# First layer: where a borrowed PSUM bank's piece is copied out, and the next one begun, in slots 5 and 6

## The chip, the cores and the metric

One core of a Trainium2 chip runs the whole program: TensorE (PE in the profile), VectorE (DVE), ScalarE (ACT), GpSimd (POOL) and the DMA queue of SyncE (SP). The metric is the device time of one execution in microseconds (us). The kernel before took 17000.62 us, the median of three runs (16998.64 to 17003.07).

## The reference

Eight images of 48 x 48 x 96 pass four layers; each layer adds its output to its input, after a group norm of the input. Cut to what matters:

```
def step(h, inp):                       # layers 0, 2 and 3: a selective scan along the pixels
    u, dl, Bv, Cv = inp
    dA = jnp.exp(dl[..., None] * A)
    h = h * dA + (dl * u)[..., None] * Bv[:, :, None, :]
    y = jnp.einsum('bkdn,bkn->bkd', h, Cv)
    return (h, y)
...
h = jnp.transpose(_upsample_rfft(xc), (0, 2, 3, 1))   # layer 1: a pointwise MLP on twice the resolution
h = h @ W1.T + b1
h = coef[:, 0] + coef[:, 1] * h + coef[:, 2] * (h * h)
h = h @ W2.T + b2
...                                                    # low pass, every second pixel
x = x + _L0_conv_ref(_gn(x), ...)
x = x + _L1_conv_ref(_gn(x), ...)
x = x + _L2_conv_ref(_gn(x), ...)
x = x + _L3_conv_ref(_gn(x), ...)
```

In each scan layer an image is read in four directions, with 192 channels and 16 states.

## The kernel before, in words

**Stages.** `ss2d("l0")` computes layer 0, `lines` layer 2, `ss2d("l3")` layer 3. Layer 1, the MLP, has no stage of its own. It is a *guest* (class `Guest`): a generator (`items`) cuts it into small pieces, and the pieces are worked off beside layers 0 and 2 as soon as an image of layer 0 is done.

**Blocks, turns and slots.** A direction of an image is cut into five blocks of 480 or 384 pixels, so a scan layer has 8 x 4 x 5 = 160 blocks. A block has four turns (0 to 3), and a turn has two slots, so a block has slots 0 to 7. Each turn runs three scans on DVE (`scan`, L337), of two groups of 128 rows each. A scan needs the products that DVE or POOL made (`make_dbu`, L305) and a pair of exponentials that ACT wrote to PSUM (`make_da`, two ACTIVATEs of L329 for one scan). The PSUM buffers of these pairs are two, so ACT can be at most one pair ahead of the scan in work. After a scan, POOL multiplies the states (`make_hc`, L343), and PE sums them (`reduce`, L363 and L365).

**The order is written out by hand.** The program turns the scheduler off (`manual_schedule`): each engine runs its instructions in the order in which the code issues them. In turn t the loop of `scans` issues: scan of pair 0, exponentials of pair 1, scan of pair 1, exponentials of pair 2, the copy of B to PSUM for an odd slot (`copy_b`, L286), the first `aside`, then `begin`, `make_hc`, *the first pair of exponentials of the next turn*, scan of pair 2, another `copy_b`, and the second `aside`. In turn 3 the next turn is turn 0 of the next block.

**What an aside does.** `aside(at)` (L407 to L425) first lets the guest *settle*: ACT copies out of PSUM what the pieces begun in the slot before have left there. Then it issues loads, a step of the side work (`side`: the convolution that prepares the next image, or the layer norm and output of the last one), the stage steps of the block that comes next (`stage1`), and at last `guest.turn`.

**The guest's turn** (L1022) issues DMAs whose time has come, earns one credit a slot (two at most), and begins one piece for each credit and free PSUM bank: PE matmuls now, the ACT copy put on a list (`put`) for the next settle. In layer 0 two banks can be free (L766):

```
guest.banks = lambda slot, clear: (["side"] if clear else []) + (["s1"] if slot in (2, 5, 6) else [])
```

The bank `side` belongs to the side work and is lent when that is between two steps (`clear`). The bank `s1` belongs to the stage steps, which use it so in each block: step `s0` in slot 7 (PE, L721), its copy in slot 1 (ACT, L726), `raw` in slots 3 and 4 (PE, L711), `biased` in slots 4 and 5 (ACT, L715). In slot 6 comes the Softplus (ACT, L739), with a table load before it and one before the exponentials that follow. So `s1` is lent in slots 2, 5 and 6.

**Pieces and their lines** (PE, then the ACT copy of its result): raising the height L1145 and L1147; `widen` L1174 and L1176; `hidden` L1181 and L1183; `narrow` L1192 and L1194, of 18 matmuls or of 12; `slim` L1203 and L1200; `lower` L1235, L1237 and L1240.

Of the kernel before, what the change touches and what calls it, by code (L numbers as in the profile page):

```python
# [29 lines left out]
NG = 8  # L30
# [72 lines left out]
def vss_stack_kernel(ctx: ExitStack, tc: tile.TileContext, i: dict, out: bass.AP):  # L103
# [120 lines left out]
    def scans(dirs, order, restart, on_pool, a, pools, ps, stage1, opening, done, side, tail, ahead=None, guest=None):  # L224
# [30 lines left out]
        def load_dd(b, half):  # L255

            t = pools["dd"].tile([P, 3 * 2 * WMAX], F32, tag="dd", name="dd")
            nc.sync.dma_start(t[:, :6 * b.m], b.dd[half].unsqueeze(1).to_broadcast([32, 4, 6 * b.m]))
            b.got[half] = t[:, :6 * b.m].rearrange("p (g t m) -> p g t m", g=3, t=2)

        def load_bc(t):

            b, slot = blocks[t // NG], t % NG
            sg = ORDER[slot][1]
            other = t - slot + NG - 1 - slot
            n = min(free, key=lambda n: free[n])
            free[n] = other
            r = bufs[n]
            rows4 = b.bcd[8 * sg:8 * sg + 8, :].rearrange("(s w) n -> s (w n)", w=2)
            nc.sync.dma_start(r[:, LEAD:LEAD + 2 * b.n], rows4.unsqueeze(0).to_broadcast([32, 4, 2 * b.n]))  # L270

            lo, hi = LEAD - b.at.start, LEAD + b.n
            bcs[t] = bcs[other] = r[:, lo:hi + b.at.start], r[:, hi:hi + b.n]
# [17 lines left out]
        def make_dbu(t, engine):  # L291

            if t >= NG * len(blocks):
                return
            b, slot = blocks[t // NG], t % NG
            if t // 2 not in dbus:
                dbus[t // 2] = rooms[t // 2 % (NG // 2)]
            cut = 3 - on_pool.get(slot, 0)
            lo, hi = (0, cut) if engine is nc.vector else (cut, 3)
            if lo == hi:  # L300
                return
            o = units(dbus[t // 2], b, 3 * (slot % 2) + lo, 3 * (slot % 2) + hi)[:, :, b.by]
            du = b.got[ORDER[slot][0]][:, lo:hi, 1, b.by]
            by = (bps[t] if engine is nc.vector else bcs[t][0])[:, b.by]
            engine.tensor_mul(o, du, by.unsqueeze(1).to_broadcast([P, hi - lo, by.shape[1]]))  # L305
# [13 lines left out]
        def make_da(t, pair):  # L319
            if t >= nt:  # L320
                return
            b, q = turns[t]
            da = ps("da", 2, 1024)
            das[t, pair] = da
            for u in (2 * pair, 2 * pair + 1):
                half, sg = ORDER[2 * q + u // 3]
                ci = half * 12 + sg * 3 + u % 3
                at = (u - 2 * pair) * b.m
                nc.scalar.activation(da[:, at:at + b.m], b.got[half][:, u % 3, 0, :], AF.Exp, scale=a[:, b.k, ci:ci + 1])  # L329

        def scan(t, pair):
            b, q = turns[t]
            da = das.pop((t, pair))[:, :2 * b.m]
            db = dbus[t][:, 2 * pair * b.m:(2 * pair + 2) * b.m]
            if b.back:
                da, db = da[:, ::-1], db[:, ::-1]
            nc.vector.tensor_tensor_scan(db, da, db, 0.0, ALU.mult, ALU.add)  # L337

        def make_hc(t, sub):
            b, q = turns[t]  # L340
            n = b.n
            h = units(dbus[t], b, 3 * sub, 3 * sub + 3)[:, :, b.at]
            nc.gpsimd.tensor_mul(h, h, bcs.pop(2 * t + sub)[1].unsqueeze(1).to_broadcast([P, 3, n]))  # L343

        def finish(at):
            while ends:
                b, half = ends.pop()
                for n, step in done(b, half, ys.pop((b, half))):
                    later.setdefault(at + n, []).append(step)

        def reduce(t, sub):

            b, q = turns[t]
            n = b.n
            half, slot = q // 2, 2 * (q % 2) + sub
            if slot == 0:
                ys[b, half] = ps("y", 1)
                lhsT, rhs = opening(b, half)
                nc.tensor.matmul(ys[b, half][:, :n], lhsT=lhsT, rhs=rhs, start=True, stop=False)  # L359
            y = ys[b, half]  # L360
            hc = units(dbus[t], b, 3 * sub, 3 * sub + 3)
            for g in range(3):
                nc.tensor.matmul(y[32 * g:32 * g + 32, :n], lhsT=wc["red"][:, :32], rhs=hc[:, g, b.at], start=False, stop=(slot == 3))  # L363

            nc.tensor.matmul(y[DH:, :n], lhsT=wc["red"][:, 32:], rhs=hc[:, 2, b.at], start=False, stop=(slot == 3))  # L365
            if slot == 3:
                ends.append((b, half))
            if sub == 1:
                dbus.pop(t)
# [3 lines left out]
        def plan(b, at):  # L373
            b.got = {}
            sources(b, pools)
            for n, step in stage1(b).items():
                steps.setdefault(at + n, []).append(step)

        def run(t):
            for step in steps.pop(t, []):  # L380
                step()
# [25 lines left out]
        def aside(at):  # L407

            nblk, slot = at // NG + 1, at % NG
            if guest:  # L410
                guest.settle()
            if nblk < len(blocks):
                for n, of in enumerate(LOAD_BC):
                    if of == slot:
                        load_bc(NG * nblk + n)
                if slot in load_in:
                    load_dd(blocks[nblk], load_in.index(slot))
            clear = next(beside, True)
            run(at)
            for step in later.pop(at, []):  # L420
                step()
            while tail:
                tail.pop(0)()
            if guest:
                guest.turn(slot, clear)  # L425

        for t, (b, q) in enumerate(turns):
            at, nblk = 2 * t, t // (NG // 2)
            if q == 0:
                if nblk + 3 < len(blocks):  # L430
                    plan(blocks[nblk + 3], at + NG)
                if b.k == order[0] and b.first:
                    beside = side(b.job)
            scan(t, 0)
            if t > 0:
                make_hc(t - 1, 1)
            make_dbu(at + 2, nc.vector)
            make_da(t, 1)
            make_dbu(at + 2, nc.gpsimd)
            make_dbu(at + 3, nc.gpsimd)  # L440
            if t > 0:
                reduce(t - 1, 0)
            scan(t, 1)
            make_da(t, 2)
            copy_b(at + 3)
            make_dbu(at + 3, nc.vector)
            if t > 0:
                reduce(t - 1, 1)
            aside(at)
            begin(t + 2)  # L450
            make_hc(t, 0)
            make_da(t + 1, 0)
            scan(t, 2)
            copy_b(at + 4)
            finish(at + 1)
            aside(at + 1)
            if q == NG // 2 - 1 and b.k == order[-1] and b.last:
                for _ in beside:
                    while tail:
                        tail.pop(0)()  # L460
# [534 lines left out]
    class Guest:  # L995
# [15 lines left out]
        def tile(self, shape, name):  # L1011
            return self.pool.tile(shape, F32, tag=f"g_{name}", name=f"g_{name}")

        def settle(self):
            while self.pending:
                self.pending.pop(0)()

        def put(self, p, step, behind):
            step(p)
            self.pending.append(lambda: behind(p))  # L1020

        def turn(self, slot, clear):  # L1022
            ready, self.soon = [f for n, f in self.soon if n <= 1], [(n - 1, f) for n, f in self.soon if n > 1]
            for step in ready:
                step()
            self.credit = min(self.credit + self.rate, 2.0)
            if self.wait:
                self.wait -= 1
                return
            banks = self.banks(slot, clear)  # L1030
            while True:
                self.item = self.item or next(self.work)
                kind, *of = self.item
                if kind == "idle":
                    self.item = None
                    return
                if kind == "wait":
                    self.item, self.wait = None, of[0] - 1
                    return
                if kind == "do":  # L1040
                    self.item = None
                    of[0]()
                    continue
                if not banks or self.credit < 1.0:
                    return
                self.item = None
                self.credit -= 1.0
                self.put(self.psum(banks.pop(0)), *of)

        def items(self):  # L1050
            room = self.room
# [206 lines left out]
    guest = Guest(stack, x1, x2)  # L1258
# [98 lines left out]
```

## Time and profile before

| | |
|---|---|
| median of the runs | 17000.62 us (16998.64 to 17003.07) |
| the profiled execution, its own time | 17010.73 us |
| its span, first to last instruction | 17007.9 us |
| mean granted TensorE clock | 0.854 |
| layer 0 with guest pieces beside it | about 1250 to 5755 us of the span |

The page gives each engine's busy time and the groups of instructions by line. "Idle before" is the time in which that engine stood idle just ahead of the group's instructions, with what ended it. A timeline lists instructions in order of time: start, length, engine, line, operation, output and inputs, shape, how many follow each other, and in brackets the idle time before. Reductions (L363, L365) are left out below where they say nothing.

### The profile page before, as it was taken

The numbers are of one execution on the slowest core, as the hardware profiler recorded it, in microseconds if no ns is written. First come the engines' busy times: TensorE is split into PE (matmuls) and PEld (weight loads), VectorE is DVE, ScalarE is ACT, GpSimd is POOL, SyncE is SP. The second block draws the span as 40 slices with busy tenths as digits, with TensorE's granted clock in tenths as the row PEclk, the third lists the DMA queues.
The fourth block names the chain that finished last, engine by engine and source line by source line (L and its number), as shares of the span: only waits on it lengthen the run. The fifth ranks groups of instructions, "written<-read, shape, count | busy, mean of one in ns | idle before, by whom it ended". The sixth has DMA issues, their size and how long they took to land.

```text
span 17007.9 us, 172189 instructions
## 1 busy us (share of the span) xinstructions
PE 13000.3 (76%) x53740; PEld 4643.6 (27%) x53740; DVE 15774.2 (93%) x9680; ACT 13824.5 (81%) x20812; POOL 15185.0 (89%) x7999
## 2 busy tenths in 40 slices
PE   6778887888787777777777777776777777777776
PEld 1223232333332333233323332221222222222221
DVE  7999999999999799999999999997999999999998
ACT  6878878888787688888888888886877878878876
POOL 7998989998889788888888888887999999999998
PEclk7878888889898789889989998887888878878887
DMA  4555555564555444544454444444545455555554
GB/s 149 180 170 172 180 163 182 171 185 169 173 172 179 141 153 167 167 161 164 158 171 159 158 166 160 160 156 139 180 168 181 173 170 176 176 172 176 175 176 143
DMA packets 931143, 2844.03 MB, mean 167 GB/s; under 512 B 396668, under 2 KB 464988, under 8 KB 803406
## 3 DMA queue, kind: packets, MB, share of 16 engines
q1 hardware_dynamic: 930222, 2833.03, 49.9%
q8 instruction: 422, 6.91, 0.2%
q14 instruction: 499, 4.09, 0.1%
HBM read 2384.40 MB, written 448.17 MB: 167 GB/s over the span
## 4 chain that ended last, share of the span: by engine, by line
POOL 24%; DVE 22%; ACT 21%; issue 18%; PE 10%; DMA 3%; SPq 1%; POOLq 0%; DVEq 0%; ACTq 0%
DVE dbu L337 15%; POOL dbu L343 14%; ACT ps_da L329 8%; POOL dbu L305 7%; DVE dbu L305 6%; ACT L329 3%; POOL dds L507 3%; PE ps_y L363 2%; ACT ps_b L286 1%; DMA bc<-bcd 1%; DMA dd<-dds 1%; PE ps_side L582 1%; PE ps_s L711 1%; ACT L739 1%; PE ps_sb L874 1%
## 5 line engine op out<-in xcount | busy, mean ns | idle before, releaser
L337 DVE TENSOR_TENSOR_SCAN dbu<-ps_da,dbu 128x968 f32<-128x968 f32 (+3 forms) x5760 | 11822.8, 2075 | 782.2 <-ACT ps_da L329 644.7
L343 POOL TENSOR_TENSOR dbu<-dbu,bc 128x1440 f32<-128x1440 f32 (+1 forms) x3840 | 10065.4, 2635 | 1486.5 <-DVE dbu L337 948.7
L329 ACT ACTIVATE ps_da<-dd,w_l_a 128x484 f32<-128x484 f32 (+3 forms) x11520 | 7419.0, 649 | 2395.5 <-DVE dbu L337 2166.1
L363 PE MATMUL ps_y<-dbu,w_red 128*32 128x480 f32 (+1 forms) x23040 | 4282.5, 658 | 1806.8 <-POOL dbu L343 1744.4
L365 PE MATMUL ps_y<-dbu,w_red 128*32 128x480 f32 (+1 forms) x7680 | 4242.3, 658 | 0.0
L305 DVE TENSOR_TENSOR dbu<-dd,ps_b 128x962 f32<-128x962 f32 (+5 forms) x2720 | 3810.3, 1401 | 186.2 <-ACT ps_b L286 137.7
L305 POOL TENSOR_TENSOR dbu<-dd,bc 128x481 f32<-128x481 f32 (+3 forms) x2080 | 3883.9, 1883 | 0.0
L363 PEld LDWEIGHTS ps_y<-dbu,w_red 128*32 128x32 f32 x23040 | 708.5, 118 | 5244.5 <-POOL dbu L343 3767.7
L286 ACT COPY ps_b<-bc 128x482 f32<-128x482 f32 (+2 forms) x2560 | 1364.6, 533 | 116.5 <-DVE dbu L305 104.1
L582 PE MATMUL ps_side<-xpad,w_l_cw 128*128 128x480 f32 (+1 forms) x2880 | 1323.1, 597 | 46.7 <-ACT g_room L1183 16.4
L329 ACT ACT_TABLE_LOAD x993 | 1274.0, 1283 | 17.4
L711 PE MATMUL ps_s<-bcl,square 128*128 128x480 f32 (+1 forms) x1280 | 874.3, 773 | 231.3 <-ACT dds L715 82.6
L359 PE MATMUL ps_y<-big,eye 128*128 128x480 f32 (+1 forms) x960 | 745.5, 865 | 254.2 <-ACT big L762 249.7
L721 PE MATMUL ps_s<-big,square 128*128 128x480 f32 (+1 forms) x1280 | 844.5, 790 | 66.4 <-ACT g_room L1183 18.0
L507 POOL TENSOR_TENSOR dds<-dds,big 96x960 f32<-96x960 f32 (+1 forms) x320 | 706.7, 2209 | 123.3 <-ACT dds L739 120.4
L582 PEld LDWEIGHTS ps_side<-xpad,w_l_cw 128*128 128x128 f32 x2880 | 559.8, 205 | 789.3 <-issue 671.9
L874 PE MATMUL ps_sb<-xpad,square 128*128 128x480 f32 (+1 forms) x1280 | 613.6, 626 | 46.9 <-ACT g_room L1183 22.8
L365 PEld LDWEIGHTS ps_y<-dbu,w_red 128*32 128x32 f32 x7680 | 647.5, 117 | 0.0
L874 PE MATMUL ps_sa<-xpad,square 128*128 128x480 f32 (+1 forms) x1280 | 521.3, 548 | 0.0
L917 PE MATMUL ps_sa<-xpad,square 128*128 128x480 f32 (+1 forms) x320 | 251.5, 881 | 342.1 <-ACT g_room L1183 109.7
L762 ACT COPY big<-ps_y 96x480 f32<-96x480 f32 (+1 forms) x640 | 471.7, 737 | 39.0 <-PE ps_y L365 37.6
L711 PEld LDWEIGHTS ps_s<-bcl,square 128*128 128x128 f32 x1280 | 249.6, 239 | 759.5 <-ACT dds L715 327.2
(250 smaller groups left out, 12525.4 us busy)
## 6 DMA issues: line engine op xcount, KB each, us to landing
dd<-dd SPq DMA_DIRECT2D x512, 1452.0 KB
bc<-bcd SPq DMA_DIRECT2D x1536, 480.0 KB
dd<-dd SPq DMA_DIRECT2D x256, 1440.0 KB
dd<-dds SPq DMA_DIRECT2D x1536, 121.0 KB
dd<-dd SPq DMA_DIRECT2D x128, 1164.0 KB
bc<-bcd SPq DMA_DIRECT2D x384, 384.0 KB
dd<-dds SPq DMA_DIRECT2D x768, 120.0 KB
dd<-dd SPq DMA_DIRECT2D x64, 1152.0 KB
```

The source lines that it names most:

```text
L286: nc.scalar.copy(bps[t][:, :bcs[t][0].shape[1]], bcs[t][0])
L305: engine.tensor_mul(o, du, by.unsqueeze(1).to_broadcast([P, hi - lo, by.shape[1]]))
L329: nc.scalar.activation(da[:, at:at + b.m], b.got[half][:, u % 3, 0, :], AF.Exp, scale=a[:, b.k, ci:ci + 1])
L337: nc.vector.tensor_tensor_scan(db, da, db, 0.0, ALU.mult, ALU.add)
L343: nc.gpsimd.tensor_mul(h, h, bcs.pop(2 * t + sub)[1].unsqueeze(1).to_broadcast([P, 3, n]))
L363: nc.tensor.matmul(y[32 * g:32 * g + 32, :n], lhsT=wc["red"][:, :32], rhs=hc[:, g, b.at], start=False, stop=(slot == 3))
L365: nc.tensor.matmul(y[DH:, :n], lhsT=wc["red"][:, 32:], rhs=hc[:, 2, b.at], start=False, stop=(slot == 3))
L507: nc.gpsimd.tensor_mul(du, dt, u)
L582: nc.tensor.matmul(pu[:, :n], lhsT=flat[:, at:at + P], rhs=xpad[:, r0 + dy:r0 + dy + nr, dx:dx + W], start=(tap == 0), stop=(tap == 8))
L711: nc.tensor.matmul(got["p"][:, :n], lhsT=wide("dtw", (2 * b.k + half) * DH), rhs=b.bcl[:, :n], start=True, stop=True)
L721: nc.tensor.matmul(got["p"][:, :n], lhsT=wide("xp", (2 * b.k + half) * NBC), rhs=uall[:, half], start=(half == 0), stop=(half == 1))
L874: nc.tensor.matmul(got["u", half][:, :n], lhsT=wide("cw", at), rhs=shifted(off), start=(tap == 0), stop=(tap == 3))
```

## The change

Only layer 0 is touched, since the new branches need a guest and `restart` false; layer 2 has `restart` true, and layer 3 has no guest.

- In slot 6, `aside` settles all pending copies except those of the bank `s1`. It returns without the guest's turn, and hands `clear` to the loop.
- In the same turn (turn 3), after `begin`, `make_hc` and `make_da(t + 1, 0)`, the loop settles the rest (the copy of a piece begun in `s1` in slot 5), and then runs the guest's turn of slot 6.
- `put` takes the bank's name and keeps it beside the copy, so that `settle` can tell which to hold.

```
 def aside(at):
     if guest:
-        guest.settle()
+        guest.settle(("s1",) if slot == 6 else ())
...
+    if guest and slot == 6 and not restart:
+        return clear
     if guest:
         guest.turn(slot, clear)
...
-    aside(at)
+    clear = aside(at)
     begin(t + 2)
     make_hc(t, 0)
     make_da(t + 1, 0)
+    if guest and at % NG == 6 and not restart:
+        guest.settle()
+        guest.turn(6, clear)
     scan(t, 2)
     copy_b(at + 4)
...
-def settle(self):
-    while self.pending:
-        self.pending.pop(0)()
-
-def put(self, p, step, behind):
+def settle(self, held=()):
+    now = [step for bank, step in self.pending if bank not in held]
+    self.pending = [(bank, step) for bank, step in self.pending if bank in held]
+    for step in now:
+        step()
+
+def put(self, bank, step, behind):
+    p = self.psum(bank)
     step(p)
-    self.pending.append(lambda: behind(p))
+    self.pending.append((bank, lambda: behind(p)))
```

More of the change, by code (lines that the diff above doesn't have):

```diff
@@ L1047, in turn @@
                 self.credit -= 1.0
-                self.put(self.psum(banks.pop(0)), *of)
+                self.put(banks.pop(0), *of)
         def items(self):
```

## The prediction

> **What bounds the kernel now.** I read the page first, then sums by stretch, then the timelines of single blocks.
>
> ```profile
> PE 13000.3 (76%) x53740; PEld 4643.6 (27%) x53740; DVE 15774.2 (93%) x9680; ACT 13824.5 (81%) x20812; POOL 15185.0 (89%) x7999
> ...
> L337 DVE TENSOR_TENSOR_SCAN dbu<-ps_da,dbu 128x968 f32<-128x968 f32 (+3 forms) x5760 | 11822.8, 2075 | 782.2 <-ACT ps_da L329 644.7
> ```
>
> DVE is busy for 93% of the span, and more than half of its idle time (782.2 of some 1234 us) lies before scans; the exponentials on ACT end most of that. The same by stretch, the second being layer 0 with guests:
>
> ```profile
> 1310.00:5750.00 4440.00, 3611.91 (x16335) 1463.73 (x16334) 4069.17 (x2503) 3645.39 (x5725) 3974.26 (x2266) 0.86 0.54 173
> ```
>
> The columns are PE, PE weight loads, DVE, ACT, POOL, the granted clock, DMA. DVE idles 371 us, ACT 795, POOL 466: DVE sets the pace, and what holds DVE up is what can be won. Sorting the scans of layer 0 by their place in the block (counted over the trace's scan records), of the twelve, the first scan of turn 0 carries 154.5 us of idle, the first of turn 2 53.6, the first two of turn 3 50.3 and 44.9, the second of turn 0 16.4, the rest 34.5 together. All 104 idles over 0.2 us at turn 0's first scan end within 0.1 us after its exponentials, so ACT is behind each, also where another releaser is printed. One such block, ACT and then DVE:
>
> ```profile
> 4953.50 0.54 ACT L286 COPY ps_b<-bc 128x482 f32<-128x482 f32 x1
> 4954.10 0.40 ACT L1194 COPY g_room<-ps_s 73x288 f32<-73x288 f32 x1
> 4954.52 1.28 ACT L739 ACT_TABLE_LOAD   x1
> 4955.81 1.00 ACT L739 ACTIVATE dds<-dds 96x960 f32<-96x960 f32 x1
> 4956.83 1.28 ACT L329 ACT_TABLE_LOAD   x1
> 4958.13 1.37 ACT L329 ACTIVATE ps_da<-dd,w_l_a 128x484 f32<-128x484 f32 x2
> 4959.43 0.54 ACT L286 COPY ps_b<-bc 128x482 f32<-128x482 f32 x1
> 4959.91 0.31 ACT L1194 COPY g_room<-ps_s 73x192 f32<-73x192 f32 x1
> 4960.13 1.37 ACT L329 ACTIVATE ps_da<-dd,w_l_a 128x484 f32<-128x484 f32 x2
> ```
>
> ```profile
> 4956.02 2.17 DVE L337 TENSOR_TENSOR_SCAN dbu<-ps_da,dbu 128x968 f32<-128x968 f32 x1
> 4959.53 2.17 DVE L337 TENSOR_TENSOR_SCAN dbu<-ps_da,dbu 128x968 f32<-128x968 f32 x1 [1.34 <-ACT ps_da L329]
> 4961.62 1.13 DVE L305 TENSOR_TENSOR dbu<-dd,ps_b 128x962 f32<-128x962 f32 x1
> 4962.66 4.23 DVE L337 TENSOR_TENSOR_SCAN dbu<-ps_da,dbu 128x968 f32<-128x968 f32 x2
> ```
>
> In slot 6 ACT does a guest copy, a table load, the Softplus, another table load and the pair, in that order. DVE is free at 4958.19 and gets its pair at 4959.50. The guest copy is the one part of this row that turn 0 does not need. PE in the same block (the piece of slot 5 is the 18 matmuls, that of slot 6 the 12):
>
> ```profile
> 4951.92 2.14 PE L1192 MATMUL ps_s<-g_w2q,g_room 128*128 128x96 f32 x18
> ...
> 4957.97 1.30 PE L1192 MATMUL ps_s<-g_w2q,g_room 128*128 128x96 f32 x12
> 4959.11 1.48 PE L582 MATMUL ps_side<-xpad,w_l_cw 128*128 128x384 f32 x4
> ```
>
> Today slot 6's piece runs while ACT is at the pair, and its copy at 4959.91 finds it done.
>
> **Part 1: the copy goes behind the pair (a gain).** Here ACT is free at 4954.04 and starts the table load at 4954.52: 0.48 us. The pair then ends at 4959.02, DVE waits 0.86 instead of 1.34. I counted this over all blocks: 89 of the 160 have such a copy from `s1` in slot 6. In 73 of them the scan waits, 116.3 us in all. What the copy takes away (from the end of ACT's earlier work to the start of the next, so with its wait for PE), capped by the scan's wait, is 62.9 us: 34.2 us in 19 blocks where the copy waits over 0.3 us for its piece on PE (three of them 3.7 to 4.0 us, a narrow piece at half clock), and 28.7 us in 54 blocks of about 0.53 us (copies of 0.33 to 0.67). Where the scan that frees the pair's buffer ends too late for that, its end is the cap; such cases are in the count.
>
> **Part 2: slot 6's piece waits for that copy (a loss).** Both use the bank `s1`, so PE can begin the piece only after ACT has read the old one, hence after the pair. The settle of slot 7 then stands on ACT until PE is done, and behind it stands the second pair of turn 0. In the block above: the held copy runs 4958.95 to 4959.35, the 12 matmuls 4959.4 to 4960.7, their copy from 4960.75; 0.22 us later (as 4959.91 to 4960.13 now) the pair of 1.37 starts, done at 4962.34. DVE starts turn 0 at 4959.05 and wants that pair 3.13 us later (4959.53 to 4962.66 now), at 4962.18. It goes on at 4962.37 instead of 4962.66: of the 0.48 won 0.29 is left. A block with the 18 matmuls in slot 6 comes out worse:
>
> ```profile
> 3458.71 0.65 ACT L1176 ACTIVATE g_room<-ps_s,g_shift,g_rs 96x365 f32<-96x365 f32 x1
> ...
> 3462.99 1.37 ACT L329 ACTIVATE ps_da<-dd,w_l_a 128x484 f32<-128x484 f32 x2
> ```
>
> The copy's 0.67 us brings the pair's end from 3464.36 to 3463.69. The held copy ends 3464.2, the piece (2.14 us) 3466.4, the pair 3468.15; DVE now starts that scan at 3467.53. Net 0.66 us lost. Both blocks break even at a piece of about 1.5 us on PE. Full-clock pieces take 0.78 (`hidden`), 0.82 (`lower`), 1.01 (`slim`), 1.07 (`widen`), 1.30 and 2.14 (`narrow`).
>
> The same arithmetic, over the 73 blocks, with each piece's own PE time:
> - 14 blocks have no `s1` piece in slot 6: won 17.0, given back 2.3 (the held copy pushes the rest of slot 7).
> - 44 have a short one (mean 0.88 us): won 31.6, given back 15.4.
> - 8 have the 12 matmuls: won 10.3, given back 7.4.
> - 7 have the 18: won 4.0, given back 10.4.
> - The 16 blocks without a wait lose 0.3.
>
> Sum: 62.9 - 35.8 = 27 us won. A delay of 0.1 us from ACT's end to PE's start is inside it. The trace does not show the reordered handoff; its nearest rows start PE 0.05 us after an ACT copy. Another 0.1 us a block takes 4 us off, 0.1 less adds 3. I take one step of 0.1 us dearer, for weight loads that now wait too: 24 us with rounding.
>
> **The rest of what moves.** Ahead of the moved turn now go on POOL `make_hc` and `begin`, which makes them earlier than the guest's few POOL operations; a gain of nothing, as POOL was waiting 3.44 us for DVE just before. Queue SP: no DMA is issued between the old place of the turn and the new, so its order is the same. PE: no instruction is issued in between either; but while PE waits for the copy, the convolution of slot 7 (1.48 us), `s0` (1.77) and the first reductions stand behind it. In the block above they start some 1.6 us late, at 4960.7 instead of 4959.11; `s0` then ends about 4964.0, and its copy on ACT comes at 4967.11. At half clock that cover of 3 us is used up; three blocks in the count have a narrow piece of over 3 us in slot 6, at up to 2 us each: 0 to 6 us, inside the range. The `copy_b` behind the held copy goes 0.45 us later, and its reader on DVE comes over 2 us after. Pieces in the bank `side` keep their copies where they were.
>
> The granted clock reads 0.86 in this stretch, half or full from moment to moment, and PE now idles before slot 6's piece, about 1.3 us in the first block and 2 in the second. The extreme, from rows of this trace: with every such piece at the longest time seen of its kind (`hidden` 1.06, `widen` 1.88, `slim` 1.83, `narrow` 2.60 and 4.16 us, `lower` taken as 1.60, twice its time), the sum is 20 us lost instead of 27 won. I keep the pieces' own times, in which the half-clock stretches of this run already are. A rule that speaks against the change stands in "TensorE: Matmul & The Clock Gate" of the Trainium skill (What's actually happening): an idle window of about 3.4 us halves the clock. By it, if the new idle tipped each of these windows, the sum would be that extreme; if it tipped none, nothing.
>
> **The rivals.**
> 1. *Nearly all of the 63 us stays* (16938 to 16960). That needs ACT's stall in slot 7 to be covered: DVE would have to have other waits there. Against it: the second scan of turn 0 waits for ACT in few blocks today (16.4 us in all), so DVE wants that pair on time.
> 2. *Nothing moves* (about 17000). POOL would have to be the real pace: it is on the chain of waits with 24%, DVE with 22. Against it: POOL stands idle for DVE 3.44 us in the first block, 2.93 in the second, right before slot 6, and the gain per block is a fifth of that.
> 3. *Slower.* Mechanism: ACT's wait in slot 7 for the piece begun late. Price: 4 to 6 us for each 0.1 us that PE's start or run is longer in the blocks counted. It decides from 0.55 us a block, where the 27 are gone; at 0.8 us it is 14 us slower (17015), at half clock throughout 20 (17021), with PE's backlog of 6 on top 17027.
>
> **How the numbers follow.** The sum is against the profiled execution (17010.7 us, 10 above the median); differences are carried to the median of 17000.6. Likeliest, 0.57: about half is given back, 17000.6 - 24 = 16976, own range 16955 to 16998 (the two ends of the handoff delay, and the backlog). Rival 1: 0.18. Rival 2: 0.09. Rival 3: 0.16. What a measurement of this kernel tells from no change is about 0.2%, 34 us: under 16967 counts as faster, which takes rival 1 and a sixth of the likeliest, 0.28; over 17035 lies beyond what rival 3 adds up to, 0.06 for a stall that I don't see; the rest is 0.66. The range leaves out the best third of rival 1 and the worse half of rival 3: 16945 to 17014.
>
> **What the profile after would show.** The idle before turn 0's first scan falls from 154.5 us to about 92; that before its second scan rises from 16 to some 50. ACT copies of `narrow` and `hidden` from `s1` in slot 7 get waits for PE that are not there now. Guest pieces by count and bank stay the same. I am wrong if the first does not fall, if the second stays flat, or if DVE's time goes to a wait on POOL or on a `side` step.

## The result, and the profile after

The changed kernel takes 17027.69 us (median of 22 runs, 17020.61 to 17034.9) where the kernel before takes 17005.95 us (22 runs beside it): the ratio is 1.0013, with a 95% interval of 1.0007 to 1.0018, so some 12 to 31 us slower. 24 us faster was forecast.

The page of the changed kernel, busy time and the scans:

```profile
PE 13006.9 (76%) x53740; PEld 4671.1 (27%) x53740; DVE 15776.6 (93%) x9680; ACT 13835.9 (81%) x20813; POOL 15183.8 (89%) x7999
...
L337 DVE TENSOR_TENSOR_SCAN dbu<-ps_da,dbu 128x968 f32<-128x968 f32 (+3 forms) x5760 | 11828.8, 2077 | 791.0 <-ACT ps_da L329 667.1
```

DVE's busy time is the same within 3 us, and the idle before its scans has risen a little, 782.2 to 791.0 us. Sorted by place in the block over layer 0's 160 blocks, that small sum hides two large terms (idle of DVE in us, added up from the trace's DVE records; two executions of each kernel, the second ones from the experiments below). Side steps are the subtractions, copies and the like that DVE does for the side work:

| place in the block | before | before, again | changed | changed, again |
|---|---|---|---|---|
| first scan of turn 0 | 154.5 | 151.9 | 95.3 | 93.6 |
| second scan of turn 0 | 16.4 | 16.3 | 60.7 | 57.2 |
| the ten other scans | 183.3 | 180.4 | 210.8 | 193.8 |
| side steps after the third scan of turn 0 | 40.1 | 42.6 | 52.5 | 56.2 |
| layer 0, first scan to layer 2's first | 5740.5 | 5731.3 | 5761.7 | 5744.7 |

In the other two scan layers the idle before scans differs by less than 8 us with both signs. So the gain came (59 us on average at the first scan) and was given back in three places: 43 us at the second scan, 20 at later scans, 13 at side steps. Lines of the changed kernel are shifted: `narrow` is L1200 with its copy L1202, `hidden` L1189 and L1191, the copy of `widen` L1184, `s0` L726, the convolution L587, the layer norm's mean L616 (L611 before) and its subtraction L619 (L614).

The second block of the prediction (a `widen` in slot 5, the 18 matmuls of `narrow` in slot 6). Kernel before, PE and then DVE:

```profile
3462.36 2.14 PE L1192 MATMUL ps_s<-g_w2q,g_room 128*128 128x96 f32 x18
3464.34 1.80 PE L582 MATMUL ps_side<-xpad,w_l_cw 128*128 128x480 f32 x4
3465.99 1.77 PE L721 MATMUL ps_s<-big,square 128*128 128x480 f32 x4
...
3464.39 2.17 DVE L337 TENSOR_TENSOR_SCAN dbu<-ps_da,dbu 128x968 f32<-128x968 f32 x1 [2.19 <-ACT ps_da L329]
3466.48 1.13 DVE L305 TENSOR_TENSOR dbu<-dd,ps_b 128x962 f32<-128x962 f32 x1
3467.53 4.23 DVE L337 TENSOR_TENSOR_SCAN dbu<-ps_da,dbu 128x968 f32<-128x968 f32 x2
```

Changed kernel, ACT:

```profile
3473.55 1.37 ACT L329 ACTIVATE ps_da<-dd,w_l_a 128x484 f32<-128x484 f32 x2
3474.86 0.64 ACT L1184 ACTIVATE g_room<-ps_s,g_shift,g_rs 96x365 f32<-96x365 f32 x1
3475.40 0.56 ACT L286 COPY ps_b<-bc 128x482 f32<-128x482 f32 x1
3477.83 0.40 ACT L1202 COPY g_room<-ps_s 73x288 f32<-73x288 f32 x1 [1.88 <-PE ps_s L1200]
```

PE:

```profile
3475.55 2.25 PE L1200 MATMUL ps_s<-g_w2q,g_room 128*128 128x96 f32 x18 [1.88 <-ACT g_room L1184]
3477.63 1.80 PE L587 MATMUL ps_side<-xpad,w_l_cw 128*128 128x480 f32 x4
3479.28 1.77 PE L726 MATMUL ps_s<-big,square 128*128 128x480 f32 x4
```

DVE:

```profile
3474.95 2.17 DVE L337 TENSOR_TENSOR_SCAN dbu<-ps_da,dbu 128x968 f32<-128x968 f32 x1 [1.60 <-ACT ps_da L329]
3477.04 1.13 DVE L305 TENSOR_TENSOR dbu<-dd,ps_b 128x962 f32<-128x962 f32 x1
3479.53 2.17 DVE L337 TENSOR_TENSOR_SCAN dbu<-ps_da,dbu 128x968 f32<-128x968 f32 x1 [1.36 <-ACT ps_da L329]
```

Read them from top to bottom. The held copy now follows the pair (3474.86). PE has waited 1.88 us for it and begins the piece at 3475.55. ACT then stands 1.88 us for PE. The first scan's wait has gone from 2.19 to 1.60, the second's from 0 to 1.36. PE's convolution and `s0` stand behind the piece, and end later against the scans than they did: `s0` ended 3.4 us after the start of the first scan, now 6.1 us after it.

What that last sentence costs is plainest where the side work is the layer norm and the clock is low. One such block, kernel before, `s0` and the subtraction that waits for the layer norm's mean:

```profile
5065.78 1.88 PE L721 MATMUL ps_s<-big,square 128*128 128x480 f32 x4 [0.58 <-ACT g_room L1194]
...
5072.39 1.15 DVE L614 TENSOR_TENSOR big<-big,ps_side 96x960 f32<-96x960 f32 x1
```

Changed kernel, PE (of the piece's 18 matmuls the window holds 12):

```profile
5087.60 2.77 PE L1200 MATMUL ps_s<-g_w2q,g_room 128*128 128x96 f32 x12
5090.86 3.57 PE L726 MATMUL ps_s<-big,square 128*128 128x480 f32 x4 [0.49 <-ACT g_room L1202]
...
5097.84 1.88 PE L616 MATMUL ps_side<-big,mean 128*128 128x480 f32 x4
```

and DVE:

```profile
5092.11 4.24 DVE L337 TENSOR_TENSOR_SCAN dbu<-ps_da,dbu 128x968 f32<-128x968 f32 x2 [3.27 <-ACT ps_da L329]
5099.75 1.15 DVE L619 TENSOR_TENSOR big<-big,ps_side 96x960 f32<-96x960 f32 x1 [3.41 <-PE ps_side L616]
```

`s0` took 3.57 us instead of 1.88, the mean of the layer norm came late, and DVE stood a second time, 3.41 us, for the side step. In the kernel before this subtraction started with no wait.

Sorted by block (idle of DVE in us, the mean of the two changed profiles less that of the two before), the loss lies in the 89 blocks after a held copy:

| blocks | first scan | second scan | ten others | side steps |
|---|---|---|---|---|
| 73: copy held in `s1`, slot 6 begins a piece there | -42 | +40 | +9 | +12 |
| 16: copy held, no piece begun in `s1` | -16 | +3 | +9 | 0 |
| the 71 others | 0 | 0 | +2 | +1 |

So half of what later scans lose comes where no piece is begun late. There it is `s0`, which writes to `s1` too, that waits for the held copy: PE stands for guest copies ahead of `s0` 21 and 20 us in these 16 blocks (10 times), and not at all in the two profiles before. One of them, changed kernel (there `s0` started in the kernel before with no wait, 1.3 us ahead of the first scan):

```profile
3230.48 3.46 PE L726 MATMUL ps_s<-big,square 128*128 128x480 f32 x4 [2.97 <-ACT g_room L1191]
3233.87 1.87 PE L1182 MATMUL ps_side<-g_upt,g_room 48*96 48x73 f32 x10
...
3235.78 0.66 ACT L1184 ACTIVATE g_room<-ps_side,g_shift,g_rs 96x365 f32<-96x365 f32 x1 [1.58 <-PE ps_side L1182]
...
3238.25 1.77 DVE L337 TENSOR_TENSOR_SCAN dbu<-ps_da,dbu 128x776 f32<-128x776 f32 x1 [1.70 <-ACT ps_da L329]
```

PE begins `s0` 2.97 us late, the `widen` behind it ends late, ACT stands for that, and DVE's first scan of turn 1 stands for ACT.

### The profile page after: what moved, and what is told of

Read it like the earlier page. It is cut to its first block, busy times and chain, and to the rows that moved or that the text cites. A ratio compares the mean times of both kernels' runs of the same rounds, so it can differ in the third digit from the quotient of the medians.

```text
span 17026.0 us, 172187 instructions
## 1 busy us (share of the span) xinstructions
PE 13006.9 (76%) x53740; PEld 4671.1 (27%) x53740; DVE 15776.6 (93%) x9680; ACT 13835.9 (81%) x20813; POOL 15183.8 (89%) x7999
## 4 chain that ended last, share of the span: by engine, by line
POOL 27%; ACT 20%; DVE 20%; issue 17%; PE 11%; DMA 3%; SPq 1%; POOLq 0%; DVEq 0%; ACTq 0%
POOL dbu L343 16%; DVE dbu L337 13%; POOL dbu L305 7%; ACT ps_da L329 7%; DVE dbu L305 5%; ACT L329 3%; POOL dds L512 3%; PE ps_y L363 2%; DMA dd<-dds 1%; ACT ps_b L286 1%; DMA bc<-bcd 1%; PE ps_s L726 1%; PE ps_side L587 1%; PE ps_s L716 1%; ACT L744 1%
## 5 line engine op out<-in xcount | busy, mean ns | idle before, releaser
L337 DVE TENSOR_TENSOR_SCAN dbu<-ps_da,dbu 128x968 f32<-128x968 f32 (+3 forms) x5760 | 11828.8, 2077 | 791.0 <-ACT ps_da L329 667.1
L587 PE MATMUL ps_side<-xpad,w_l_cw 128*128 128x480 f32 (+1 forms) x2880 | 1342.7, 605 | 47.0 <-ACT g_room L1191 16.9
L726 PE MATMUL ps_s<-big,square 128*128 128x480 f32 (+1 forms) x1280 | 853.9, 798 | 59.0 <-ACT g_room L1191 16.0
L587 PEld LDWEIGHTS ps_side<-xpad,w_l_cw 128*128 128x128 f32 x2880 | 568.4, 208 | 803.3 <-issue 690.5
L922 PE MATMUL ps_sa<-xpad,square 128*128 128x480 f32 (+1 forms) x320 | 248.9, 872 | 341.5 <-ACT g_room L1191 109.7
```

Source lines behind the costliest of these rows:

```text
L587: nc.tensor.matmul(pu[:, :n], lhsT=flat[:, at:at + P], rhs=xpad[:, r0 + dy:r0 + dy + nr, dx:dx + W], start=(tap == 0), stop=(tap == 8))
L726: nc.tensor.matmul(got["p"][:, :n], lhsT=wide("xp", (2 * b.k + half) * NBC), rhs=uall[:, half], start=(half == 0), stop=(half == 1))
```

## The experiments

Theory A: the loss is the handoff of `s1`, that is slot 6's piece begun late, ACT behind it, and the work that is queued behind it on PE. Theory B: what the changed profile shows in later places is scatter of the TensorE clock between executions, or the late copy itself. Theory A' adds that the clock falls in front of the late piece.

**The same two programs again (no edit).**

> The kernel before, profiled a second time, to see how much the idle times of layer 0 differ between two executions of the same program. Theory A (the 22 us come from slot 6's piece that waits for the held copy, and from what stands behind it on PE and ACT): the idle before scans repeats, 154 us within 6 before turn 0's first scan, 16 within 4 before its second, and the ten other places together within 8 of the first profile (183 us). Theory B (what the changed kernel's profile shows in the later places is the scatter of the TensorE clock from run to run): the ten other places differ by 20 us or more.

This execution took 16995.74 us, beside a median of 16997.39 us for 21 others of the same kernel. Its page:

```profile
L337 DVE TENSOR_TENSOR_SCAN dbu<-ps_da,dbu 128x968 f32<-128x968 f32 (+3 forms) x5760 | 11818.3, 2074 | 772.6 <-ACT ps_da L329 635.0
```

The places repeat within 3 us each (table above), where theory B needs 20. Layer 0 as a whole differs by 9 us here and by 17 us between the two profiles of the changed kernel, so a difference of that size between two single profiles says little.

> The changed kernel, profiled a second time. Theory A': what stands against the gain is the piece begun late, and part of its price is TensorE's clock, which falls to half in front of it because PE idles there. Then as in the first profile of the changed kernel some 15 to 20 of the 72 late pieces run at half clock (5 in the first profile before and 3 in the second), PE's time in them is 9 to 14 us above the kernel before, and the second scan of turn 0 idles 57 to 65 us, the later scans 200 to 215. Rival C: the half-clock pieces in the changed profile were chance; then 3 to 9 of them here, and the second scan at 45 to 52 us.

17014.83 us, a single execution (the kernel before has a median of 16997.63 us beside it). The second scan idles 57.2 us, the side steps 56.2; the later scans 193.8, below the 200 that I gave, and still above both profiles before. Take each of the 73 blocks whose `s1` has both a held copy and a piece after it (the prediction's 73 are others: those where the first scan waits), and compare the later piece's time on PE with the full-clock time of its kind (0.78 to 2.14 us; a piece close to the limit can fall either way, so each count is good to one):

| | over 1.25 of the full-clock time | above it in all, us | PE idle just before, mean us |
|---|---|---|---|
| before | 7 of 73 | 6.6 | 0.0 |
| before, again | 4 | 5.1 | 0.0 |
| changed | 19 | 18.5 | 1.23 |
| changed, again | 16 | 14.7 | 1.10 |
| turn moved, nothing held (below) | 3 | 3.7 | 0.0 |

So slow pieces are no chance (rival C falls): they come with the idle in front of them, and cost some 11 us of PE time (8 to 13 by single pairs). The granted clock tells when it fell. Of the 19 and 16 slow pieces 3 each met a clock that was at half before the idle began, as 3 did in each profile before; in 7 and 3 it fell within the idle, and in 9 and 10 only within the piece (4 and 2 before). Theory A' has the price right; that the clock falls ahead of the piece holds for the smaller part.

**No piece behind a held copy.** Slot 6 lends `s1` only if nothing is held there; the MLP of the last image leaves out bands 7 to 14 of 15.

```
-                guest.settle()
-                guest.turn(6, clear)
+                taken = any(bank == "s1" for bank, _ in guest.pending)
+                guest.settle()
+                guest.turn(6, clear, ("s1",) if taken else ())
...
-            banks = self.banks(slot, clear)
+            banks = [bank for bank in self.banks(slot, clear) if bank not in taken]
...
```

> The changed kernel, but slot 6 lends the bank s1 only if no copy is held in it, so that no piece waits for a held copy. The guest is slower by that; to let it end in time the MLP of the last image leaves out bands 7 to 14 of 15. What counts is layer 0 (up to some 5750 us), which the left-out work does not touch. Theory A: idle before turn 0's first scan about 92 us, before its second about 17, the later places as in the kernel before; layer 0 some 55 to 65 us shorter than before, 75 to 85 shorter than changed. Theory B: the first scan 92, the second 17, but the later places stay some 25 us above the kernel before; layer 0 about 35 shorter than before.

16922.32 us, ratio 0.9954 (0.994 to 0.9968). The first scan idles 90.0 us, the second 17.9, the ten others 166.7, side steps 39.0; layer 0 is 5659.0 us, 77 below the mean of the two profiles before, more than the 55 to 65 that I gave. Its page:

```profile
L337 DVE TENSOR_TENSOR_SCAN dbu<-ps_da,dbu 128x968 f32<-128x968 f32 (+3 forms) x5760 | 11817.1, 2074 | 698.8 <-ACT ps_da L329 585.8
```

ACT's waits for `narrow` in `s1`, in the stretch of layer 0 with guests (total us, times, longest), in this kernel, in the changed one and in the one before:

```profile
ACT g_room L1203 <- PE ps_s L1201: 13.3, 10, 3.0
...
ACT g_room L1202 <- PE ps_s L1200: 46.9, 25, 5.4
...
ACT g_room L1194 <- PE ps_s L1192: 49.4, 31, 5.5
```

Between changed and before the sum hardly differs, but the place does: over all pieces in `s1`, ACT waits 42 and 36 us for those begun in slot 5 in the two profiles before and 6 in the changed ones, and for those begun in slot 6 it waits 21 and 20 us before and 77 and 76 changed. With no piece behind the held copy, the second scan is back at its old idle and the later places are below it: theory A, not B. `s0` still waits for held copies, but all its waits for guest copies add up to 55.5 us over the layer, where the two profiles before have 51.5 and 53.7. Part of the 77 us may not be the order's: layer 0 holds 658 copies of guest pieces here and 708 in the kernels before and changed, and work is left out in layer 2 (more below).

**No narrow piece behind a held copy.** Short pieces are still begun there; the narrow ones carry a mark.

```
...
-                if not banks or self.credit < 1.0:
+                if not banks or self.credit < 1.0 or banks[0] in taken and len(of) > 2:
                     return
...
```

> The changed kernel, but where a copy is held in s1, slot 6 does not begin a narrow piece (12 or 18 matmuls) in that bank; short ones are begun as in the changed kernel. Theory A: of the 21 blocks that had narrow there, what they lost goes (20.9 us before the second scan and 14 in later places, in the changed kernel's trace), some of it replaced by other pieces: idle before the second scan 35 to 45 us instead of 61, total 16995 to 17010. Theory B: total within 8 us of the changed kernel's 17028.

16988.51 us beside 16997.39 before: 0.9991 (0.9982 to 1.0), 9 us below before, which the interval does not tell from none, but below the changed kernel's 1.0013, and 6 us under the range that I gave. The second scan idles 36.2 us, the others 190.0, side steps 40.4. Of the 58 late pieces that are left 7 run slow. So the long pieces carried over half of what the second scan had lost, and the side steps' loss as well; layer 0 holds 692 guest copies here, 16 fewer.

**The side step ahead of the late piece.** Slot 6's piece is begun in slot 7, after the PE work of slot 7's side step and before `s0`.

```
...
             clear = next(beside, True)
+            if late:
+                guest.more(["s1"])
+                guest.settle()
             run(at)
...
```

> The changed kernel, but slot 6's piece in s1 is begun in slot 7, behind the PE work of slot 7's side step and ahead of s0; the held copy stays where the change put it, and slot 6's piece in the bank side goes back to its old place. So the side step no longer stands behind a PE that waits. Theory A: the wait of DVE for side steps after the third scan of turn 0 falls from 52 to about 41 us, the later places lose some 20 to 25 us against the changed kernel, the second scan's idle stays at 55 to 70 us; total 16995 to 17012. Theory B: later places as in the changed kernel, total 17020 to 17035.

17020.24 us, again 1.0013 (1.0005 to 1.0022). The later scans idle 181.9 us and the side steps 40.0, both as before the change. That is what theory A says of these places, if the backlog on PE made their losses; but the second scan now idles 89.3 us, well over the 70 that I gave, and the product on DVE ahead of it another 6.8, and a DVE that comes later can find the later places ready for that reason alone. The total lies 8 us above what I gave, where theory B had put it. Layer 0 also holds 727 guest copies here, 19 more. So this run agrees with the backlog and does not isolate it; the table by block does that better. ACT's waits in layer 0 with guests, this kernel, the two longest for `narrow` (L1207) and one for `hidden` (L1196):

```profile
ACT g_room L1209 <- PE ps_side L1207: 105.0, 51, 7.4
ACT g_room L1209 <- PE ps_s L1207: 51.7, 26, 4.0
ACT g_room L1198 <- PE ps_s L1196: 36.1, 29, 6.8
```

Added up over layer 0, ACT waits for PE 352 to 368 us in the two profiles before, 420 to 439 in those of the change, 459 here, and 312 where no piece is begun behind a held copy. And `s0`, which now stands behind the piece and its copy, waits for guest copies 109.7 us over the layer (51.5 and 53.7 before). Whichever work PE does first, the other waits.

**The turn alone.** Slot 6's settle copies everything at its start again; only the guest's turn stays behind the pair.

```
-                guest.settle(("s1",) if slot == 6 else ())
+                guest.settle()
```

> The change with one part undone: slot 6's settle copies everything at its start again, held copies included, and only the guest's turn of slot 6 is issued behind the pair. Theory A': moving the turn alone does nothing, since no PE or DMA instruction is issued between its old place and its new one; the first scan of turn 0 idles 150 to 156 us, the second 14 to 19, total within 8 us of the kernel before. Rival E (the moved turn itself costs, through the order of POOL or of the loads): 10 us slower or more, with the first scan at 154.

17003.48 us beside 17002.64: 1.0 (0.9991 to 1.0009). First scan 150.3 us, second 16.4:

```profile
L337 DVE TENSOR_TENSOR_SCAN dbu<-ps_da,dbu 128x968 f32<-128x968 f32 (+3 forms) x5760 | 11822.7, 2075 | 772.4 <-ACT ps_da L329 636.0
```

The place of the turn costs and gives nothing. Gain and loss both come from holding the copy, with what then waits for it.

**No piece in slot 5 at all.** The kernel before with one word changed; the last image leaves out bands 7 to 14.

```
-(["s1"] if slot in (2, 5, 6) else [])
+(["s1"] if slot in (2, 6) else [])
```

> The kernel before with one word changed: slot 5 does not lend s1. No copy is held and no turn is moved; slot 6 begins its piece in s1 at the old place. As the guest is slower, the MLP of the last image leaves out bands 7 to 14 of 15. Theory A' (the gain is worth having wherever the copy ahead of the pair goes, and holding it is not what matters): layer 0 as in the run that held the copy and lent s1 only if free, 5655 to 5675 us from its first scan to layer 2's, first scan of turn 0 about 90 us idle, second 16 to 20, total 16915 to 16935. Rival D (the gain there came from a piece that finds its bank free in slot 6 no more often, that is from less PE work in slot 6): layer 0 5690 us or more.

16976.69 us, 0.9987 (0.9978 to 0.9996). First scan 93.7 us, and second 21.5, near what theory A' gives; but layer 0 takes 5696.8 us, 38 more than where copies were held, with 64.1 us at the side steps (39.0 there) and 49.1 before the second scan of turn 3 (33.1). The total is missed by 42 us. Layer 0 above 5690 was the mark of rival D: of the 77 us of the run that held copies, some 39 come without holding any, with about as few guest copies in layer 0 (657 and 658); the rest is not explained. The pieces are other ones in other slots here; which of them holds up the side steps I have not separated.

**Whole computations with part of it.** Copies held and `s1` lent only if free, in blocks 0 to 79, and in another kernel (`at >= 100 * NG`) in blocks 100 to 159; elsewhere the order of the kernel before.

```
-                guest.settle(("s1",) if slot == 6 else ())
+                guest.settle(("s1",) if slot == 6 and at < 80 * NG else ())
...
-            if guest and at % NG == 6 and not restart:
+            if guest and at % NG == 6 and at < 80 * NG and not restart:
+                taken = any(bank == "s1" for bank, _ in guest.pending)
...
```

> The whole computation. In the first 80 of the 160 blocks of layer 0: copies from s1 are held behind the pair, and slot 6 lends s1 only if none is held; in the other 80 blocks the order of the kernel before. Theory A': the first 80 blocks gain as in the run that did so in all blocks (81 us over 160 blocks there, 89 of which had a held copy, 36 of them in the first 80), so some 30 to 40 us; total 16957 to 16972 against a before of about 17000. Theory B (the gain of that run came from the pieces that were left out or put off, not from the order): no more than 10 us.

> The whole computation. As the run over the first 80 blocks, but in blocks 100 to 159 instead: copies from s1 are held behind the pair there, and slot 6 lends s1 only if none is held; the order of the kernel before in blocks 0 to 99. Theory A': these 60 blocks took 2192 us in the run that did so in all blocks, against 2244 and 2242 us in the two profiles of the kernel before, so 35 to 50 us gained, total 16948 to 16965 against a before of about 17000. Theory B (that run gained there because earlier blocks had put pieces off): no more than 15 us.

Blocks 0 to 79: 16977.71 us beside 16997.63, 0.9987 (0.9978 to 0.9996); first scan 118.1 us, second 16.4. These blocks take 2770 us where the two profiles before have 2794 and 2787, as much as in the run that held copies in all blocks (2770). Blocks 100 to 159: 16975.86 us beside 17002.64, 0.9984 (0.9975 to 0.9993); first scan 119.3 us, second 15.5; 2218 us in these blocks against 2244 and 2242 before and 2192 in the run over all blocks. Both gain 20 to 27 us, less than theory A' gives and more than theory B does: I split the 81 us of the full run in proportion. 17 to 24 us in the first 80 blocks, some 25 in the last 60 and 5 in the 20 between leave some 26 of the 77 us, all in the last 60 blocks. The full run has no fewer guest copies there than the run over these blocks (306 and 295; 322 before), so the number of pieces put off does not explain them, and their cause stays open. Both kernels compute everything and are faster than the kernel before and the changed one. But the guest does less in layer 0 in both (683 and 681 copies), and the run that lends no `s1` in slot 5, and holds nothing, takes 2764 us in blocks 0 to 79 and 2220 us in 100 to 159. So what is shown is that the pair without a copy ahead of it gains; that holding the copy gains more than not having one there is not.

## Why the prediction was wrong

- *What bounds the kernel: right.* DVE's wait for turn 0's first pair could be won: 154.5 to 95.3 and 93.6 us, with 92 forecast.
- *Part 1, the gain of 62.9 us: right.* Over the blocks it measures 59 to 66 us (each changed profile against each before), from the start of the scan ahead to the first scan of turn 0.
- *Part 2, the mechanism right, the term too small.* I priced it at 35.8 us (the second scan at some 50 us). The second scan's idle rises by 41 to 44 us. The prediction took each piece's own time on PE from the profile before. The wait makes PE idle 1.1 to 1.2 us ahead of the piece on average, and 16 to 19 of 73 pieces then run over 1.25 times their full-clock time instead of 4 to 7. "TensorE: Matmul & The Clock Gate" of the Trainium skill (What's actually happening) had the warning, an idle window of about 3.4 us that halves the clock; all but 2 and 1 of the 73 idles here are shorter than that. The slower pieces cost some 11 us of PE time, and the term came out 5 to 9 us short, far from the 47 between my two extremes. A smaller slip: `lower` was priced at 0.82 us, but its piece has two matmuls of L1235 ahead of those, 1.45 us in all in the profile before; in the 5 blocks that have it this is 3 us.
- *The step that failed: "The rest of what moves", PE.* It put the work queued behind the waiting piece at 0 to 6 us, and at nothing in the sum of 24, from one full-clock block in which `s0` had 3 us of cover. Measured are 10 to 30 us at later scans and 10 to 16 at side steps (each changed profile against each before). The table by block puts nearly all of this where a copy is held: 9 us at later scans and 12 at side steps in the 73 blocks with a piece begun late, and 9 us at later scans in the 16 where only `s0` waits. The timelines show the chain from PE's wait to DVE's. Taking the side step out of that queue takes both places back to their old idle and puts the wait on the second scan instead. I looked for the next reader of `s0` only, and left out that ACT's other copies and DVE's layer-norm steps read what PE does behind the piece; and in the blocks without a piece I counted what the held copy pushes on ACT, not that `s0` needs the same bank.
- *Rival 3* had the right sign and named ACT's wait in slot 7 and the backlog. By its own price, 4 to 6 us for each 0.1 us, pieces that take some 11 us longer over 73 blocks (0.15 us each) cost 6 to 9 us and not the 27 that it needs; the backlog, which it put at 6 us, made the rest. That its 17027 is near the measured 17027.69 is luck: the kernel before measured 5 us longer than the 17000.62 from which it counts. The forecast's sign of being wrong, DVE's time going to a side step, did show: 13 us. Rival 2 is excluded by the runs that gain 20 us and more from the same wait; rival 1 by the second scan.
- *The rest: right.* No DMA, no POOL operation matters; the turn moved alone measures 1.0.

By the means of two profiles each, the four terms (-59, +43, +20, +13) add up to 17 us, within the interval of 12 to 31 that the runs give.

## What to carry to other kernels

If a copy out of a shared PSUM bank is put off, the next use of that bank is put off with it, and where each engine works in the order of issue everything queued behind that use is late too: list every next user of the bank (here the late piece, and `s0` where there was none), and price the whole queue, on the engine that waits and on those that read from it, not the moved instruction alone. A put-off copy paid where no further piece was put between it and the bank's next fixed user: holding it and not lending the bank again, over parts of layer 0, measured 0.9987 and 0.9984 of the whole program's time, with less guest work in that layer. Piece times taken from a trace hold only for the idle time that the trace has in front of them.

## What the runs showed of the hardware that I had not expected

A mean idle of 1.1 to 1.2 us ahead of short PE pieces was enough to make some three times as many of them run at a lowered clock (16 to 19 of 73 instead of 4 to 7), while the granted clock of the whole stretch stayed at 0.86 and the half-clock share of time went only from 27 or 28% to 28 or 29%. In 9 and 10 of the slow pieces the granted clock fell only after the piece had begun. With the side step's matmuls put into that gap (mean idle 0.4 us) 13 of 77 were slow.
